# Layer 2's expert weights made beside layer 1's gathers, and layer 1's shared expert ahead of its routed experts

## The chip, the cores and the metric

The kernel runs on one core of a Trainium2 chip. The metric is the device time of one execution in microseconds (us). TensorE (PE, with its weight loads as PEld), VectorE (DVE), ScalarE (ACT), GpSimd (POOL) and SyncE (SP, which only issues DMAs) have a queue of instructions each and run side by side. All data is float32.

## The reference, cut to what matters

Four layers follow each other on an activation `x` of 4 x 1024 tokens with 128 features; each has a mixing part ("attn") and a feed-forward part ("ffn"), and a layer norm follows each part. What this case touches:

```python
# layer 1, ffn: 16 experts, 4 chosen for each token, and a shared expert of width 256
h = jnp.einsum('td,edf->etf', x, gate_w)
u = jnp.einsum('td,edf->etf', x, up_w)
y = jnp.einsum('etf,efd->etd', jax.nn.silu(h) * u, down_w)
routed = jnp.einsum('etd,te->td', y, combine)
sh = jax.nn.silu(x @ sh_gate_w) * (x @ sh_up_w) @ sh_down_w
return (routed + sh).reshape(hidden_states.shape)
...
# layer 2, ffn: 8 experts share w_gate, w_up, w_down; each adds a product of rank 16 to each of them
d1 = jnp.einsum('enr,efr->enf', jnp.einsum('nd,erd->enr', x, A1), B1) * SCALE
act = jax.nn.silu(common_w1[None] + d1) * (common_w3[None] + d3)
```

Layer 1's mixing part is a linear recurrence over 1024 steps with 128 complex states (`l1_attn` in the kernel), layer 0's ffn a product with values rounded to six bits (`l0_ffn`), layer 2's mixing part causal attention with 16 heads (`l2_attn`).

## The kernel before

The tokens lie in 32 tiles of 128, in four quarters of the sequence with 8 tiles each; `x` and its transpose `xT` stay in SBUF. The four layers are worked on for parts of the sequence. First the first half (quarters 0 and 1) goes through layer 0 and the mixing part of layer 1: `l0_attn((0, 1))`, `l0_ffn((0, 1))`, `l1_attn((0, 1))`. Then its route is computed (`l1_route`), and GpSimd scatters its rows with 64 indirect DMAs into a list in DRAM that is sorted by expert (`spread`), while `l0_attn((2, 3))` works on the second half. Layer 1's ffn of the first half follows, with `l0_ffn` and `l1_attn` of the second half as side work. Then comes `l2_attn(0)`.

The ffn of layer 1 has four pieces:
- `l1_wall` loads the 16 experts' weights, 3 MB, into one tile `wall` (line 153, the DMA issue `ld<-in_l_w` of SP).
- `l1_experts` (`small_experts`) runs over 20 groups of four tiles of the sorted list: SP loads the rows (`xg`, L1324), TensorE transposes them (`tp`, L165), multiplies with gate and up of the tile's expert (`gu`, L157), ScalarE and VectorE form the product (L1688, L1689), TensorE transposes it and multiplies with down (`yp`), and SP writes `yg` to DRAM (L1707).
- `l1_shared` runs over 4 blocks of 512 tokens: two pairs of matmuls `pg` and `pu` from `xT`, `down` as `py`, and an add into `x` (L822). It loads its own three weights of 128 KB each.
- `l1_close` collects, quarter by quarter: for each of 8 tiles GpSimd gathers four rows per token with four indirect DMAs (`yt`, L1293, five buffers of four), VectorE adds them into `x` with their weights (L1359), and then come the norm, a copy of `x` to DRAM (`xsave`, L832) and the transposes (`turned`). A gather reads rows of the whole list, so the first one waits for the last `yg`.

`l1_attn` takes one quarter after the other: two matmuls `pu` from `xT`, four products on VectorE (L641), two scans over 1024 columns (L645), the state that is carried on (L655 to L661), a product on GpSimd (L663; on VectorE where it runs as side work) and one on VectorE (L664), 16 pairs of matmuls `po`, two adds into `x` (L672), norm and transposes.

`l2_weights` makes the layer 2 weights of the 8 experts, three for each. It loads `l2_big` (1.5 MB) and `l2_ab` (192 KB). In each of 24 steps GpSimd multiplies `ab` with a column of 0 and 1 that picks the expert's 16 rows, and with 2 (`am`, L1399), TensorE adds the shared weight (by a matmul with the identity) and the product of rank 16 in PSUM (`pw`, printed as `s`), ScalarE copies it (`we`, L1409) and SP writes 256 KB to DRAM (`wall2`, L1411). `l2_wall` reads it back much later, from 843.67 us on.

The order of the work: each of these pieces is a generator that yields an estimate of its time. `mix(main, side)` takes a step of `main` and then as many steps of `side` as `main`'s estimates pay for; the `side` instructions on PE, ACT, DVE and POOL are put behind those of `main` that came before (`queued`). `chain` runs generators one after the other, and `abreast` takes the one whose estimates add up to least so far. When the program is built, a list scheduler fixes each engine's order from this; memory of a closed pool goes to the next ones, with waits. `self.side` is a PSUM pool of two buffers that `l2_weights`, `turned` and the side work share.

Before the change, `l2_weights` begins with its loads ahead of `l0_ffn((0, 1))`, and its 24 steps are the side work of `l1_attn((0, 1))`, with 1.0 as each step's estimate. The experts run ahead of the shared expert, which stands beside the gathers.

Of the kernel before, what the change touches and what calls it, by code (L numbers as in the profile page):

```python
# [14 lines left out]
AF = mybir.ActivationFunctionType  # L15
ALU = mybir.AluOpType
# [4 lines left out]
P = 128  # L21
# [20 lines left out]
E2, F2, R2, K2 = 8, 512, 16, 2  # L42
# [32 lines left out]
class Kernel:  # L75
# [1309 lines left out]
    def l2_weights(self):  # L1385

        nc = self.nc
        NC = F2 // P
        with ExitStack() as ctx:
            cp = self.pool(ctx, "l2wc", right=True)  # L1390
            wp = self.pool(ctx, "l2ww", 3, right=True)
            big = self.load(cp, self.ins["l2_big"])
            ab = self.load(cp, self.ins["l2_ab"])
            yield (0.0,)
            for e in range(E2):
                for i in range(3):

                    am = self.tile(wp, [P, P], "am")
                    nc.gpsimd.tensor_scalar(am, ab[:, i, :], self.cst["em"][:, e : e + 1], 2.0, ALU.mult, ALU.mult)  # L1399
                    pw = self.tile(self.side, [P, F2], "s")  # L1400
                    self.mm(pw, self.ident, big[:, i, :], True, False)
                    if i < 2:
                        self.mm(pw, am, big[:, 3 + i, :], False, True)
                    else:
                        for c in range(NC):
                            f = slice(c * P, (c + 1) * P)
                            self.mm(pw[:, f], big[:, 5, f], am, False, c == NC - 1)
                    we = self.tile(wp, [P, F2], "we")
                    nc.scalar.copy(we, pw)  # L1409
                    c0 = (e * 3 + i) * F2  # L1410
                    nc.sync.dma_start(out=self.wall2[:, c0 : c0 + F2], in_=we)  # L1411
                    yield (1.0,)

    def l2_route(self, part):
        nc = self.nc
# [393 lines left out]
    def all(self):  # L1809
        a, rest = self.first, self.rest  # L1810
        b, c = rest
        r = self.both[1]
        a2, m2, n2 = self.by_rows
        with ExitStack() as ctx:
            lgp = self.pool(ctx, "l2lg")
            self.l2_lg = self.tile(lgp, [P, NT, E2], "lg")
            with ExitStack() as early:

                self.l0_setup(early)
                self.l2_wr = self.load(lgp, self.ins["l2_wr"])  # L1820
                self.run(self.l0_attn((0, 1)))
                self.l1_setup()
                self.l2_setup()
                weights = self.l2_weights()
                next(weights)
                self.zero_lists("l1")
                self.run(self.l0_ffn((0, 1)))
                self.run(self.mix(self.l1_attn((0, 1)), weights))

                self.run(self.l1_route(a))  # L1830
                self.run(self.mix(self.l0_attn((2, 3), True), self.spread("l1", a, K1)))
                self.zero_lists("l2", "l3")
                with ExitStack() as c2:
                    wall = self.l1_wall(c2)
                    yp = self.pool(c2, "l1ya", 5, right=True)
                    side = self.chain(self.l0_ffn((2, 3), True), self.l1_attn((2, 3), True))
                    self.run(self.mix(self.l1_experts(a, wall), side, drain=False))
                    self.run(self.mix(self.chain(self.l1_shared(a), side), self.l1_close(a, yp)))
            with ExitStack() as c2:
                wall = self.l1_wall(c2)  # L1840
                self.run(self.mix(self.l2_attn(0), self.chain(self.l1_route(r), self.spread("l1", r, K1))))
                wall2 = self.l2_wall(c2)
                yp = self.pool(c2, "l1yr", 5, right=True)
                self.run(self.mix(self.chain(self.l1_experts(r, wall), self.l1_shared(r)), self.routed(a2)))
                self.run(self.mix(self.l2_experts(a2, wall2), self.l1_close(r, yp)))
            listed = lambda name: lambda: name in self.listed
            on = self.served(
                self.chain(self.rows_in(a2), self.onward(a, True)),
                (lambda: self.rows_done >= B + 2, self.routed(m2)),
                (lambda: self.rows_done == 2 * B, self.routed(n2)),  # L1850
            )
            self.run(self.mix(self.l2_attn(1), on, drain=False))
            with ExitStack() as c3:
                with ExitStack() as c2:
                    wall = self.l2_wall(c2)
                    self.press(on, listed("l2m"))
                    self.run(self.mix(self.l2_experts(m2, wall), on, drain=False))
                    self.press(on, lambda: {"l2n", "routed l3a"} <= self.listed)
                    sw, wall3 = self.l3_wall(c3, True)
                    on = self.chain(on, self.rows_in(m2))  # L1860
                    self.run(self.mix(self.l2_experts(n2, wall), on, drain=False))
                self.press(on, listed("l3a"))
                yp = self.pool(c3, "l3y", 8)
                on = self.chain(
                    on, self.rows_in(n2), self.l3_attn(b), self.l3_route(b),
                    self.abreast(
                        self.chain(self.spread("l3", b, K3), self.when(listed("made l3a")), self.last(a, yp)),
                        self.chain(self.l3_attn(c), self.l3_route(c)),
                    ),
                    self.spread("l3", c, K3), self.when(listed("made l3b")), self.last(b, yp),  # L1870
                )
                self.run(self.mix(self.chain(self.l3_shared(a, sw), self.l3_experts(a, wall3)), on, drain=False))
                self.press(on, listed("l3b"))
                self.run(self.mix(self.chain(self.l3_shared(b, sw), self.l3_experts(b, wall3)), on, drain=False))
                self.press(on, listed("l3c"))
                self.run(self.mix(self.chain(self.l3_shared(c, sw), self.l3_experts(c, wall3)), on))
                self.run(self.last(c, yp))
        bad = self.nc.values_load(self.flag[0:1, 0:1], min_val=0, max_val=1)
        with self.tc.If(bad > 0):
            with ExitStack() as ctx:  # L1880
                lgp = self.pool(ctx, "l2lg2")
                self.l2_lg = self.tile(lgp, [P, NT, E2], "lg")
                self.l2_wr = self.load(lgp, self.ins["l2_wr"])
                self.l2_attn_general()
                for p in self.by_rows:
                    self.run(self.routed(p))
                    with ExitStack() as c2:
                        self.run(self.l2_experts(p, self.l2_wall(c2)))
                    self.run(self.rows_in(p))
                for p in self.parts:  # L1890
                    self.run(self.onward(p))
                    with ExitStack() as c2:
                        sw, wall = self.l3_wall(c2)
                        self.run(self.l3_shared(p, sw), self.l3_experts(p, wall))
                        self.run(self.last(p, self.pool(c2, "l3y" + p.name, 5)))
# [165 lines left out]
```

## Time and profile before

| | us |
|---|---|
| median of 3 runs | 2137.66 (2135.64 to 2137.95) |
| the profiled execution | 2141.15 |
| its span, first to last instruction | 2139.3 |
| PE busy | 1624.2 (76%) |
| DVE busy | 1346.1 (63%) |
| ACT busy | 816.4 (38%) |
| POOL busy | 787.2 (37%) |
| `l1_attn((0, 1))` with the weights: first `pu` to second quarter's `po` | 211.4 to 280.4 |
| first and last gather of layer 1's first half | 545.48 and 633.43 |

Durations and positions come from the profiled execution, whose positions count from its first instruction; the median of the runs is 3.5 us below its own time. A row of a timeline has the start, the length, the engine, the line, the operation and what it writes and reads; the brackets give the idle time of the engine before it and what ended that. A busy TensorE is not TensorE at its peak, and idle time of an engine that nothing waits for costs nothing.

### The profile page before, as it was taken

Reading aid. Unit: us, or ns where it says so; the run is one execution under the profiler, and the core shown is the slowest. Engines: PE = TensorE matmul, PEld = TensorE weight load, DVE = VectorE, ACT = ScalarE, POOL = GpSimd, SP = SyncE. Lnnn points to the kernel's source line nnn. Section 1 sums busy time; section 2 is a strip of 40 time slices with the busy share of each in tenths; the row PEclk is TensorE's granted clock in tenths of the full one; section 3 lists DMA queues with packets and bytes.
Section 4 is the critical chain, followed back from the end, with each engine's and each line's share of the span. In section 5 each row is a group of like instructions: output and inputs, shape, how many; then the busy total and the mean of one; then the engine's idle time right before and its main releaser. Section 6 shows DMA issues by size and latency. Waiting matters only on the chain.

```text
span 2139.3 us, 28621 instructions
## 1 busy us (share of the span) xinstructions
PE 1624.2 (76%) x9605; PEld 1001.0 (47%) x9605; DVE 1346.1 (63%) x3797; ACT 816.4 (38%) x1162; POOL 787.2 (37%) x725
## 2 busy tenths in 40 slices
PE   6563967678618787989979787894989999577680
PEld 2232533367414345856633232333656688356470
DVE  8765379868666867536646667464573367568363
ACT  4621236433104344323347554661323254233240
POOL 5523218821560470535232000200226700477725
PEclk9775979789758999999999998996999999789795
DMA  9940300143320023633230000003134243144351
GB/s 323 289 126 1 118 2 35 59 137 94 127 55 11 30 111 104 222 82 85 59 114 23 1 1 1 21 1 138 50 115 148 82 122 100 37 127 127 114 147 50
DMA packets 224008, 192.05 MB, mean 90 GB/s; under 512 B 16817, under 2 KB 204081, under 8 KB 222833
## 3 DMA queue, kind: packets, MB, share of 16 engines
q1 hardware_dynamic: 203152, 147.28, 22.0%
q0 software_dynamic: 20704, 42.86, 6.5%
q8 instruction: 83, 1.36, 0.3%
q14 instruction: 69, 0.56, 0.1%
HBM read 93.47 MB, written 96.60 MB: 89 GB/s over the span
## 4 chain that ended last, share of the span: by engine, by line
PE 42%; DVE 16%; POOL 5%; issue 4%; DMA 4%; ACT 3%; SPq 0%; POOLq 0%; DVEq 0%; ACTq 0%
PE gu L157 12%; PE s L157 9%; PE sc L157 6%; PE yp L157 5%; PE tp L165 5%; POOL yt L1293 3%; PE pg L157 2%; POOL l3rc L1293 2%; PE pu L157 2%; DVE pr L1055 1%; POOL l3rb L1293 1%; PE py L157 1%; DVE x L205 1%; ACT pr L1049 1%; PE s L165 1%
## 5 line engine op out<-in xcount | busy, mean ns | idle before, releaser
L1049 ACT ACTIVATE pr<-sc 128x1024 f32<-128x1024 f32 x288 | 279.1, 1021 | 216.5 <-PE sc L157 216.5
L157 PE MATMUL gu<-ld,xgT 128*128 x768 | 195.0, 394 | 20.7 <-DVE hg L1689 12.6
L157 PE MATMUL sc<-qm,kT 32*128 32x512 f32 (+3 forms) x1536 | 190.2, 552 | 1.0 <-ACT pr L1049 1.0
L157 PE MATMUL gu<-wall,xgT 128*128 x352 | 170.8, 609 | 19.9 <-DMA wall<-wall 17.9
L157 PE MATMUL s<-pr,va 128*32 128x512 f32 (+3 forms) x1536 | 164.1, 522 | 17.7 <-DVE x L987 7.3
L157 PEld LDWEIGHTS gu<-ld,xgT 128*128 128x128 f32 x768 | 140.6, 194 | 49.7 <-ACT xgT L167 9.1
L1055 DVE TENSOR_TENSOR pr<-pr,ld 128x512 f32<-128x512 f32 (+1 forms) x160 | 92.3, 580 | 87.0 <-ACT pr L1049 86.6
L169 DVE COPY hT<-tp 128x512 f32<-128x512 f32 x140 | 95.7, 684 | 68.0 <-PE tp L165 67.8
L1689 DVE TENSOR_TENSOR hg<-sg,gu 128x256 f32<-128x256 f32 x192 | 77.9, 414 | 93.2 <-ACT sg L1688 92.8
L157 PEld LDWEIGHTS sc<-qm,kT 32*128 32x128 f32 x1536 | 83.0, 196 | 99.1 <-issue 62.6
L1462 ACT ACTIVATE sg<-gu 128x512 f32<-128x512 f32 x88 | 52.5, 598 | 199.4 <-PE gu L157 194.4
L1688 ACT ACTIVATE sg<-gu 128x256 f32<-128x256 f32 x192 | 73.2, 384 | 143.3 <-PE gu L157 115.4
L167 ACT COPY xgT<-tp 128x512 f32<-128x512 f32 x118 | 69.2, 586 | 142.8 <-PE tp L165 142.7
L165 PEld LDWEIGHTS tp<-ld,hg 128*128 128x128 f32 x736 | 91.8, 142 | 57.5 <-issue 35.8
L165 PE MATMUL tp<-ld,xg 128*128 128x128 f32 x472 | 77.7, 288 | 52.9 <-DMA xg<-l3rb 15.7
L165 PE MATMUL tp<-ld,hg 128*128 128x128 f32 x736 | 113.7, 274 | 4.5 <-DVE hT L169 2.9
L1293 POOL DMA_INDIRECT l1ra<-x,posl1a x64 | 94.4, 1476 | 60.9 <-DVE posl1a L1270 41.7
L1464 DVE TENSOR_TENSOR hg<-sg,gu 128x512 f32<-128x512 f32 x88 | 59.9, 681 | 74.8 <-ACT sg L1462 74.5
L157 PE MATMUL yp<-ld,hT 128*128 x768 | 102.7, 276 | 0.8 <-DVE hT L169 0.5
L1293 POOL DMA_INDIRECT l1rr<-x,posl1r x64 | 64.6, 1009 | 101.3 <-DVE posl1r L1270 82.1
L157 PEld LDWEIGHTS yp<-ld,hT 128*128 128x128 f32 x768 | 93.7, 192 | 1.7 <-DVE hT L169 0.9
L157 PE MATMUL yp<-wall,hT 128*128 x704 | 93.1, 275 | 1.5 <-DVE hT L169 1.5
(433 smaller groups left out, 3449.4 us busy)
## 6 DMA issues: line engine op xcount, KB each, us to landing
wall<-wall SPq DMA_DIRECT2D x16, 768.0 KB, 11.2
l3ra<-zero SPq DMA_DIRECT2D x1, 6144.0 KB
wall<-we SPq DMA_DIRECT2D x24, 256.0 KB, 2.0
ld<-in_l_w SPq DMA_DIRECT2D x2, 3072.0 KB, 13.0
ld<-in_l_w SPq DMA_DIRECT2D x1, 6144.0 KB, 19.8
xg<-l3ra SPq DMA_DIRECT2D x24, 256.0 KB, 3.8
l3ya<-yg SPq DMA_DIRECT2D x24, 256.0 KB, 2.3
l1ra<-zero SPq DMA_DIRECT2D x1, 5120.0 KB, 21.7
```

The costliest lines, as they stand in the source:

```text
L157: return self.nc.tensor.matmul(out, lhsT, rhs, start=start, stop=stop)
L165: nc.tensor.transpose(pt[:, k * P : (k + 1) * P], s, self.ident)
L167: nc.scalar.copy(dst, pt[:, : n * P])
L169: nc.vector.tensor_copy(dst, pt[:, : n * P])
L205: nc.vector.tensor_scalar(x, x, mv[:, t, 0:1], rstd[:, t : t + 1], ALU.subtract, ALU.mult)
L1049: nc.scalar.activation(pr, sc[h], AF.Exp)
L1055: nc.vector.tensor_tensor(d, d, cst["tril"].unsqueeze(1).unsqueeze(1).to_broadcast([P, 2, n, P]), ALU.mult)
L1293: ins = self.nc.gpsimd.indirect_dma_start(**kw)
L1462: nc.scalar.activation(sg, gu[:, 0, :], AF.Silu)
L1464: nc.vector.tensor_tensor(h, sg, gu[:, 1, :], ALU.mult)
L1688: nc.scalar.activation(sg, pg[:, :, 0, :], AF.Silu)
L1689: nc.vector.tensor_tensor(h[:, 2 * c : 2 * c + 2, :], sg, pg[:, :, 1, :], ALU.mult)
```

## The change

`l2_weights` leaves `l1_attn((0, 1))`. It now runs abreast of the rest of the second half's side work while `l1_close` gathers. Its masks go from GpSimd to ScalarE, with the factor 2 put into a column `em` that VectorE makes once, its pools go to the other end of the memory, and each step's estimate is 2.5 instead of 1.0. The shared expert of layer 1's first half leaves the gathers and runs ahead of the experts, in one chain with them, beside the side work.

```diff
-            cp = self.pool(ctx, "l2wc", right=True)
-            wp = self.pool(ctx, "l2ww", 3, right=True)
+            cp = self.pool(ctx, "l2wc")
+            wp = self.pool(ctx, "l2ww", 3)
             big = self.load(cp, self.ins["l2_big"])
             ab = self.load(cp, self.ins["l2_ab"])
+            em = self.tile(cp, [P, E2], "em2")
+            nc.vector.tensor_scalar(em, self.cst["em"], 2.0, None, ALU.mult)
...
-                    nc.gpsimd.tensor_scalar(am, ab[:, i, :], self.cst["em"][:, e : e + 1], 2.0, ALU.mult, ALU.mult)
+                    nc.scalar.activation(am, ab[:, i, :], AF.Copy, scale=em[:, e : e + 1])
...
-                    yield (1.0,)
+                    yield (2.5,)
...
-                weights = self.l2_weights()
-                next(weights)
                 self.zero_lists("l1")
                 self.run(self.l0_ffn((0, 1)))
-                self.run(self.mix(self.l1_attn((0, 1)), weights))
+                self.run(self.l1_attn((0, 1)))
...
-                    self.run(self.mix(self.l1_experts(a, wall), side, drain=False))
-                    self.run(self.mix(self.chain(self.l1_shared(a), side), self.l1_close(a, yp)))
+                    self.run(self.mix(self.chain(self.l1_shared(a), self.l1_experts(a, wall)), side, drain=False))
+                    self.run(self.mix(self.abreast(self.l2_weights(), side), self.l1_close(a, yp)))
```

## The prediction

> **What bounds the kernel now.** I read the page's 40 slices first, then the table by stage, the timeline at the stages' borders, the waits and the chain. The table comes first; its columns are the stretch in us, its length, then busy us (and instructions) of PE, PEld, DVE, ACT and POOL, the granted TensorE clock, the DMA share and GB/s.
>
> ```profile
> core 0: us, PE busy (x) PEld busy (x) DVE busy (x) ACT busy (x) POOL busy (x), PEclk, DMA share, GB/s
> 216.00:265.00 49.00, 48.02 (x188) 27.15 (x186) 17.16 (x40) 15.24 (x27) 12.73 (x22) 0.99 0.35 129
> 265.00:282.00 17.00, 7.54 (x48) 7.29 (x48) 13.11 (x32) 0.00 (x0) 3.33 (x1) 0.70 0.00 0
> ...
> 460.00:480.00 20.00, 18.25 (x125) 15.79 (x124) 17.22 (x59) 8.03 (x17) 2.36 (x1) 1.00 0.37 106
> ...
> 547.00:571.50 24.50, 24.50 (x105) 14.82 (x104) 8.80 (x17) 5.85 (x10) 17.77 (x19) 0.91 0.59 210
> 571.50:600.80 29.30, 9.94 (x43) 7.74 (x41) 26.61 (x89) 0.59 (x1) 21.38 (x18) 0.63 0.15 38
> 605.00:636.00 31.00, 2.27 (x8) 1.44 (x8) 11.47 (x42) 1.47 (x3) 22.36 (x24) 0.50 0.24 68
> ```
>
> TensorE is full from 216 to 265, where the weights are made; while the outputs of layer 1's experts are gathered (545 to 636) it is nearly empty but for the shared expert. The timeline shows what each stage waits for (start, length, engine, line; in brackets the idle time before and its releaser):
>
> ```profile
> 221.91 3.27 POOL L663 TENSOR_TENSOR g<-g,pw 128x1024 f32<-128x1024 f32 x1 [0.74 <-DVE l1h L660]
> 235.47 0.69 DVE L672 TENSOR_TENSOR x<-po,x 128x512 f32<-128x512 f32 x1 [10.27 <-PE po L157]
> 263.20 2.48 DVE L641 TENSOR_TENSOR b<-pu,wi 128x512 f32<-128x512 f32 x4 [15.80 <-PE pu L157]
> 274.77 5.62 PE L157 MATMUL po<-l1c,g 128*128 128x128 f32 x32 [7.51 <-POOL g L663]
> 423.19 0.33 SPq L153 DMA_DIRECT2D ld<-in_l_w  x1
> 437.47 1.99 PE L165 MATMUL tp<-ld,xg 128*128 128x128 f32 x8 [14.42 <-DMA xg<-l1ra]
> 545.48 1.02 POOL L1293 DMA_INDIRECT yt<-l1ya,posl1a  x1 [46.81 <-DMA ld<-in_l_swu]
> 576.72 2.92 POOL L1293 DMA_INDIRECT yt<-l1ya,posl1a  x1 [0.30 <-DMA yt<-l1ya,posl1a]
> ```
>
> The first and last lines will serve below. Between them: VectorE, which carries `l1_attn`, waits 10.27 us for `po` and 15.80 us for the second quarter's `pu`, both behind weight matmuls in TensorE's queue. Then TensorE waits 14.42 us for the first experts' rows. The chain of waits confirms the later bound, and shows one load that comes late behind others:
>
> ```profile
> 633.43 2.49 DMA yt<-l1ya,posl1a
> ...
> 859.76 6.33 DMA xg<-l1rr
> ```
>
> GpSimd's 64 gathers, the last at 633.43, release the norm after which `l2_attn(0)` starts.
>
> **The change, part by part.** All positions are those of the profiled execution (2141.15 us, span 2139.3).
>
> *Weights out of `l1_attn(0, 1)`.* A weight step takes four 128x512 matmuls 0.43 us apart, or two and eight of 0.11, so 1.72 to 1.75 us; 24 make 41.4 us, gone from 216 to 265. What is late next is `l1_attn`'s own chain. GpSimd's product ends at 225.2 (221.91 + 3.27), so the first quarter's `po` starts there and not at 233.5, on a cold clock (5.6 us for 32, the row at 274.77). The second quarter's `pu` needs only `xT` and the two PSUM buffers that L641 frees at 216.4; its VectorE work (2.5 for L641, 4.6 for two scans, 1.1 for the carried state) then runs from 223, with the first quarter's adds and statistics (3.6) between, to about 235. GpSimd's product adds 3.3: the second `po` starts near 238.5 instead of 274.77, **-36 us**. Everything up to the experts hangs on this chain (route, scatters, `l0_attn(2, 3)`) and moves along. Bounds: the two quarters wholly one after the other put it at 250.9 (13.1 us of tail after 225.2, then 12.6 from `pu` to `po`, as before), -24; an overlap without any loss, -38. I take -36, because before, too, instructions ready early ran early (zeroing of layer 3's lists at 75, ahead of `l0_ffn`'s weight load).
>
> *Shared expert ahead.* Its 24.3 us (547.1 to 571.4, first matmuls at half clock) should fall into the 14.4 us gap, but its weights are loaded after the 3 MB of `l1_w`, issued at 423.19 when `gate` is free. In the one-microsecond table that load moves about 400 GB/s until 433.7. In the row at 859.76 a load behind eight of 768 KB took 6.33 us against its median 3.2, so I let the 384 KB land after it, at 434.7. The shared expert then runs from 434.7 to 459, and the experts start 21.5 us later than 437.5. Bounds: its weights ahead of `l1_w`, start near 423, +10; no overlap with any wait, +24.
>
> The Trainium skill's page "DMA: Bandwidth & Descriptors", section "Queues, rings and completion order", speaks against this step: on each DMA engine the descriptors of one issuer's row are consumed in ring order. By it the gap stays empty, as I have it; a queue that shared its rate evenly would land the 384 KB about 2 us after issue and save some 9 us.
>
> *Experts and the side work.* The experts now run with the end of `side`: the shared expert's four steps advance it by 22 units, so at the experts' end 99.7 of 108 units are issued, not 77.7. Work from 435 to 600.8, summed over the table's stretches: PE 128.0 us, some 6 of it from cold clocks, so 122; DVE 122.1, less 11.1 of gathered adds and `l2_attn`'s memsets, so 111. From 460 to 530 PE was busy for 64.0 of 70 us (0.915), DVE for 60.2 (0.86). So PE gives 133 us and DVE 129: the end is at 566 to 568. Two engines that are both this full wait for each other a little more; I take 569 against 541.2, **+28 us**. Bounds: PE at 1.00 (557, +16); DVE at the whole stage's 0.79 (81.7 of 103.7; 577.5, +36).
>
> *Gathers.* They start 4.3 us after the last expert, as before (541.2, 545.48). Undisturbed, from 609.7 to 633.4, they are 1.25 us apart, 79.7 us for 64. They took 88.9: 4.0 us waiting for an add queued behind the shared expert on VectorE, the rest beside `l1_attn`'s last quarter, where single ones took 1.9 to 2.9. Both causes leave. I take 82, **-7 us** (0 to -9.2).
>
> The last timeline row is a gather of 2.92 us while VectorE scans (2.28 us, started at 576.60). The Trainium skill's page "SBUF — State Buffer", section "SBUF: two separate sides", says of the port pair that VectorE and GpSimd share that it is an exclusive lock, held for the whole instruction, so that a DMA issued by GpSimd starves for descriptors. By that rule alone only the overlapped gathers get shorter, some 5 us, not 7.
>
> *Weights beside the gathers.* 41.4 us of PE in about 82 where, without the shared expert, PE has some 13 us to do. ScalarE's mask lies between 0.302 us (128x8, L195) and 1.13 (128x1024, scaled by a column, L432), by length 0.40; with the 0.59 of the copy (L1409) 24 steps are 23.8 us on an engine busy for under 10. GpSimd, which the gathers need, gets none of it. Writes: 6.3 MB. Cost nothing; the load of 1.7 MB adds about 6 us before the first step. At half clock the steps would be 83 us and end 7 us after the gathers; before, they ran at 0.99. `em` is one 128x8 operation, about 0.16 us. The waits that are added: matmuls of `turned` and `side` share two PSUM buffers with the weights, and on SP `xsave` stands behind the weights' writes; both have 30 us to spare.
>
> *Loads off the start.* 1.7 MB less before the zeroing: nothing, as the next load, issued at 112.27, lands 18.7 us later and is read at 157.6. The 24 masks leave GpSimd (0.37 each): nobody waited but for 0.8 us.
>
> Sum: -36 + 28 - 7 = **-15 us**, 2126 us against 2141.15. The median shown, 2137.66, is 3.5 below the profiled execution: 2123.
>
> **The rivals.**
> *The gap is filled.* If the shared expert's weights land first, it starts up to 11.5 us earlier: -26, 2111. For it: their memory is free before `gate` is; against it: text order. Chance 0.13.
> *The weights were not the bound.* If the second quarter of `l1_attn` stays behind the first one's norm, the gain is 24: -24 + 28 - 7 = -3, 2135, no change. For it: at 208.5 to 211.4 `pu` of the first quarter was ready and yet waited for transposes; against it: that was a wait for memory in PSUM, which doesn't exist here. Chance 0.13.
> *The gathers lose their pace* (the slower side). Masks, copies, 24 writes and transposes now meet 64 gathers that have five buffers; if each takes what the scatters took beside a busy VectorE (L1293, 1.476 + 0.30 between), the train is 114 us, not 88.9: -36 + 28 + 25 = +17, 2155. It decides from 1.51 us per gather on, (88.9 + 8)/64; with a mean of 1.55 it is +2. Against it: scatters at 424 to 429, beside the 400 GB/s of `l1_w`, kept 1.26. Chance 0.14.
>
> **How the numbers follow.** My forecast has 0.60, its own range 2113 to 2134 (the bounds +16 to +36 narrowed by half, and some of the first term). For 8 in 10 the range takes in most of the first rival and the near part of the last: 2108 to 2142. A measurement can tell 0.2%, 4.3 us, from no change. Faster: nearly all of 0.60, the 0.13 and a little of the second rival, 0.73; the same 0.13; slower 0.14.
>
> **What would show it.** After: no `am` on POOL and no weight matmuls before 260; the second `po` near 238; the scatters, and the load of `l1_w`, 36 us earlier; the shared expert's first matmul about 11 us after that load's issue; the last expert product about 8 us earlier than 541; gathers 1.25 us apart, the last near 618; weight matmuls done some 25 us before that. I am wrong if `po` stays near 250, if the experts end later than 541, or if the gathers exceed 90 us.

## The result, and the profile after

The changed kernel takes 2141.41 us (median of 20 runs, 2132.90 to 2145.23) against 2134.47 for the one before (20 runs, 2128.01 to 2140.06): a ratio of 1.0030, 95% interval 1.0022 to 1.0039. It is slower by about 7 us; the forecast was 15 us faster.

The two first profiles seem to say the opposite: 2141.15 us for the profiled execution of before, 2136.98 for that of after. Each is untypical of its kernel, the one above all 20 timed runs, the other third from the bottom. So the stages are compared first, and a second profile of each kernel (below) tells which of them repeat. The table of after by stretches comes first, in columns like those of before:

```profile
core 0: us, PE busy (x) PEld busy (x) DVE busy (x) ACT busy (x) POOL busy (x), PEclk, DMA share, GB/s
205.00:241.00 36.00, 20.03 (x72) 13.96 (x71) 29.22 (x61) 2.65 (x5) 6.54 (x2) 0.61 0.00 0
393.00:400.00 7.00, 0.00 (x0) 0.00 (x0) 0.12 (x2) 0.00 (x0) 1.91 (x2) 0.50 0.93 375
400.00:432.00 32.00, 25.98 (x102) 15.68 (x103) 18.50 (x22) 5.36 (x9) 9.46 (x4) 0.89 0.06 17
...
605.00:629.00 24.00, 0.00 (x0) 0.00 (x0) 8.54 (x29) 0.00 (x0) 16.58 (x18) 0.50 0.19 51
629.00:640.00 11.00, 8.52 (x26) 4.85 (x26) 6.04 (x26) 2.54 (x5) 0.00 (x0) 0.68 0.42 149
```

In the first row TensorE is no longer full, as meant. In the second it does nothing for 7 us, and VectorE next to nothing (0.12 us), while DMA runs at 375 GB/s. In the row of 605 it does nothing again, for 24 us, although weights are still to be made: they are made from 629 on, when the gathers are over. The timeline of after shows why (columns as before):

```profile
207.50 6.35 PE L157 MATMUL pu<-xT,ld 128*128 128x512 f32 x8 [0.68 <-ACT xT L167]
241.00 6.63 PE L157 MATMUL po<-l1c,g 128*128 128x128 f32 x32
388.43 0.33 SPq L153 DMA_DIRECT2D ld<-in_l_w  x1
388.81 0.42 SPq L153 DMA_DIRECT2D ld<-in_l_swg  x1
400.09 2.08 PE L157 MATMUL pg<-xT,ld 128*128 128x512 f32 x2 [11.79 <-DMA ld<-in_l_swg]
435.01 1.04 PE L165 MATMUL tp<-ld,xg 128*128 128x128 f32 x8
535.14 0.50 SPq L153 DMA_DIRECT2D ld<-in_l_w  x1
538.49 0.36 SPq L1709 DMA_DIRECT2D l1ya<-yg  x1
547.06 1.02 POOL L1293 DMA_INDIRECT yt<-l1ya,posl1a  x1 [82.50 <-DMA w<-in_l_w]
590.68 0.30 ACT L195 ACTIVATE rstd<-mv,eps 128x8 f32<-128x8 f32 x1 [1.67 <-DVE mv L192]
625.81 0.94 POOL L1293 DMA_INDIRECT yt<-l1ya,posl1a  x1 [0.30 <-issue]
628.34 0.35 DVE L1359 SCALAR_TENSOR_TENSOR x<-yt,wkl1a,x 128x128 f32<-128x128 f32 x1 [0.86 <-DMA yt<-l1ya,posl1a]
629.36 2.14 DVE L205 TENSOR_SCALAR x<-x,mv,rstd 128x128 f32<-128x128 f32 x8
629.85 2.18 PE L165 MATMUL s<-ld,x 128*128 128x128 f32 x8 [36.36 <-DVE x L205]
637.62 0.59 ACT L1411 COPY we<-s 128x512 f32<-128x512 f32 x1 [1.49 <-PE s L157]
638.10 0.30 ACT L195 ACTIVATE rstd<-mv,eps 128x8 f32<-128x8 f32 x1
638.68 2.14 DVE L205 TENSOR_SCALAR x<-x,mv,rstd 128x128 f32<-128x128 f32 x8
```

Three rows of before, for comparison: the issue of the same second load of 3 MB (the last write of the experts' outputs was issued ahead of it, at 542), the last add of a gathered row, and the second quarter's norm.

```profile
544.71 0.59 SPq L153 DMA_DIRECT2D ld<-in_l_w  x1
636.01 0.35 DVE L1359 SCALAR_TENSOR_TENSOR x<-yt,wkl1a,x 128x128 f32<-128x128 f32 x1 [0.67 <-DMA yt<-l1ya,posl1a]
639.56 2.13 DVE L205 TENSOR_SCALAR x<-x,mv,rstd 128x128 f32<-128x128 f32 x8
```

Read the rows of after from the top. Both quarters' `pu` run in one go, and the second `po` comes at 241.0 and not at 274.8. The 3 MB of `l_w` are issued at 388.43 and not at 423.19. The shared expert's first weight is issued right behind them, and its first matmul waits 11.79 us for it. It then takes 31 us, to 431, so that the first experts start at 435.01, against 437.47 before: of the gain of 34 us at the last scatter (394.56 against 429.14) nearly nothing is left. Near 535 a second load of 3 MB, for the second half's experts, is issued ahead of the last write of the experts' outputs. The first gather comes 8.6 us after that write's issue; before it was 3.5 us. The brackets name `w`, a load that landed with it on the same queue; what a gather needs is the write.

The last eight rows are the end. ScalarE has the first quarter's root at 590.98, but VectorE normalises that quarter only at 629.36: in its queue the normalisation stands behind all of the second quarter's adds. TensorE has the first quarter's transposes ahead of the last two weight steps in its queue, so it waits 36.36 us; SP has that quarter's save ahead of the last three weight writes. ScalarE has the second quarter's root behind the last weight copy, so that quarter's norm comes at 638.68, 10 us after its last add at 628.34. Before, it came 3.5 us after the last add.

The next table gives the stages as differences of such rows, in us: from the second norm of layer 0 (at 155.6 before, 152.1 after) to the last scatter; to the experts' last `yp`; to the first gather; to the last one; to the first scores `sc` of `l2_attn(0)`; and their sum. The rows from the third on are the experiments.

| kernel | scatter | `yp` | first gather | last gather | `sc` | sum | ratio to before, 95% |
|---|---|---|---|---|---|---|---|
| before, two profiles | 273.5, 273.4 | 112.0, 112.0 | 4.4, 4.4 | 88.0, 88.8 | 20.2, 18.5 | 498.0, 497.1 | 1 |
| after, two profiles | 242.5, 242.1 | 143.0, 143.0 | 9.5, 9.8 | 78.8, 78.9 | 26.5, 26.0 | 500.2, 499.8 | 1.0030 (1.0022 to 1.0039) |
| weights_only | 242.4 | 111.6 | 4.5 | 105.4 | 17.3 | 481.2 | 0.9932 (0.9912 to 0.9952) |
| shared_only | 271.5 | 142.8 | 9.8 | 78.9 | 16.3 | 519.3 | 1.0155 (1.0133 to 1.0178) |
| norm_dve | 244.0 | 143.3 | 10.2 | 78.9 | 32.3 | 508.8 | 1.0058 (1.0038 to 1.0079) |
| shared_early_load | 243.1 | 131.7 | 8.5 | 78.9 | 26.9 | 489.1 | 0.9964 (0.9949 to 0.9979) |
| pace_1_5_b | 243.5 | 143.3 | 9.9 | 79.0 | 19.4 | 495.1 | 1.0009 (0.9993 to 1.0024) |
| last_write_act_b | 242.1 | 143.0 | 14.8 | 78.7 | 25.8 | 504.4 | 1.0053 (1.0033 to 1.0072) |
| early_pace_write_b | 242.2 | 129.7 | 14.6 | 79.0 | 21.7 | 487.2 | 0.9960 (0.9943 to 0.9976) |
| wall_behind | 243.3 | 141.9 | 4.3 | 78.8 | 26.3 | 494.6 | 0.9999 (0.9984 to 1.0014) |
| early_pace_behind | 244.1 | 130.1 | 4.3 | 78.8 | 21.6 | 478.9 | 0.9917 (0.9892 to 0.9942) |

### The profile page after: what moved, and what is told of

Same layout as the page of the kernel before. It is cut to its first block, busy times and chain, and to the rows that moved or that the text cites. A ratio compares the mean times of both kernels' runs of the same rounds, so it can differ in the third digit from the quotient of the medians.

```text
span 2135.1 us, 28614 instructions
## 1 busy us (share of the span) xinstructions
PE 1621.9 (76%) x9605; PEld 999.8 (47%) x9605; DVE 1352.8 (63%) x3798; ACT 823.4 (39%) x1186; POOL 767.6 (36%) x701
## 4 chain that ended last, share of the span: by engine, by line
PE 43%; DVE 16%; POOL 7%; issue 6%; DMA 4%; ACT 3%; SPq 0%; POOLq 0%; DVEq 0%; ACTq 0%
PE gu L157 12%; PE s L157 10%; PE yp L157 6%; PE sc L157 6%; PE tp L165 5%; POOL yt L1293 4%; POOL l3rc L1293 2%; DVE pr L1055 1%; POOL l3rb L1293 1%; ACT pr L1049 1%; PE pg L157 1%; PE pu L157 1%; PE s L165 1%; DVE x L205 1%; PE py L157 1%
## 5 line engine op out<-in xcount | busy, mean ns | idle before, releaser
L1293 POOL DMA_INDIRECT yt<-l1ya,posl1a x64 | 60.5, 945 | 101.7 <-DMA w<-in_l_w 82.5
```

Of the source, the lines that this page charges most:

```text
L1293: ins = self.nc.gpsimd.indirect_dma_start(**kw)
```

## The experiments

The theory from the two traces: the gain at the scatters is real; it is lost in three places, of which the forecast had only the first. The shared expert stands in the open, waiting for its weights; the gathers start behind a 3 MB load; the last weight steps stand behind the first quarter's closing in three queues. The rivals: moving the weights is itself the loss, or the end of the weights isn't on the path.

**Each part alone.** `weights_only` leaves the shared expert beside the gathers; `shared_only` is the kernel before with the shared expert ahead of the experts.

```diff
 weights_only, against after
-self.run(self.mix(self.chain(self.l1_shared(a), self.l1_experts(a, wall)), side, drain=False))
-self.run(self.mix(self.abreast(self.l2_weights(), side), self.l1_close(a, yp)))
+self.run(self.mix(self.l1_experts(a, wall), side, drain=False))
+self.run(self.mix(self.abreast(self.l2_weights(), self.chain(self.l1_shared(a), side)), self.l1_close(a, yp)))
 shared_only, against before
-self.run(self.mix(self.l1_experts(a, wall), side, drain=False))
-self.run(self.mix(self.chain(self.l1_shared(a), side), self.l1_close(a, yp)))
+self.run(self.mix(self.chain(self.l1_shared(a), self.l1_experts(a, wall)), side, drain=False))
+self.run(self.mix(side, self.l1_close(a, yp)))
```

> The weights are made beside the gathers, with ScalarE's masks, as in the changed kernel; the shared expert stays in its old place, beside the gathers too. Theory (the shared expert in the open is what eats the gain of 34 us that the last scatter shows): the scatters come some 34 us earlier than before, the experts follow at once and end near 508, and beside the gathers TensorE has 24 + 41 us of 89 to do, so the gathers stay at some 89 and a tail of up to 10 us is lost at their end. Time 20 to 30 us below before, near 2108. Rival (moving the weights is itself what loses, because they disturb the gathers and the norm behind them): less than 8 us below before, or above it.

> The shared expert goes ahead of the experts; the weights stay beside the first half's layer 1 attention, with GpSimd's masks. Theory: the shared expert costs its 24 to 31 us in the open, less about 9 us of faster gathers: 15 to 24 us above before, near 2153. Rival (the shared expert fills the gap before the first experts' rows, and so costs under 15): no more than 6 us above before. The two parts alone should add up to the whole change: with the sum far from +7 us, they share a cost.

Measured: 2117.74 us and 2163.65, before beside them 2132.64. The weights alone gain 15 us, less than the 20 to 30 of the theory, far from the rival. The shared expert alone costs 31 us, more than either expectation. The stages show both: the scatters' 31 us come with the weights, the 31 us up to `yp` with the shared expert. Together the parts give +16 by the medians, against +7 for the whole, and by the table's sums +5.3 (481.2 and 519.3 against 497.6) against +2.4. Of the 31 us of `shared_only` the table's stages hold 21.7. The rest isn't located; its profiled execution, at 2157.12 us, is the shortest of its five runs. In `weights_only` the gathers take 105.4 us, 17 more than before, since weights, shared expert and `l1_attn`'s scans now lie beside them at once:

```profile
557.56 0.94 POOL L1293 DMA_INDIRECT yt<-l1ya,posl1a  x1 [18.98 <-DVE x L1359]
566.29 2.49 POOL L1293 DMA_INDIRECT yt<-l1ya,posl1a  x1 [0.30 <-issue]
```

These two rows of its timeline are a wait of 18.98 us for a buffer, whose add stands behind the shared expert's adds in VectorE's queue, and a gather of 2.49 us beside a scan that started at 565.74. That wait alone is as long as the 17 us. So the whole is cheaper than its parts at this place, and each part's price holds only with its neighbours.

**The shared expert's weights, loaded early.** They are loaded behind `l2_setup` into a pool of their own, and passed on.

```diff
                 self.l2_setup()
+                sp = self.pool(early, "l1sw")
+                got = [self.load(sp, self.ins["l1_" + n]) for n in ("swg", "swu", "swd")]
...
-self.chain(self.l1_shared(a), self.l1_experts(a, wall))
+self.chain(self.l1_shared(a, got), self.l1_experts(a, wall))
```

> The changed kernel with one edit: the shared expert's 384 KB are loaded at the start of the kernel's second stage, into memory of their own, and not behind the 3 MB of the experts' weights. Theory (TensorE and VectorE both stand idle from 393 to 400 for these 384 KB): the shared expert's first matmul comes 6 to 9 us earlier, near 392, and all that follows with it; 6 to 9 us less than the changed kernel, near 2134. Rival (the experts' rows or weights are late anyway and eat it): within 2 us of the changed kernel, with the first experts still near 435.

Measured: 2125.24 us, 0.9964; that is 14 us less than the changed kernel by the ratios, twice what was expected, and 7 less than before. The first row of its timeline:

```profile
394.11 1.25 PE L157 MATMUL pg<-xT,ld 128*128 128x512 f32 x2
```

It stands 4.4 us ahead of the last scatter (398.55), in after 5.5 us behind it (400.09 against 394.56), so it comes 10 us sooner, where 6 to 9 were expected. The shared expert then takes 24 us, to 418, and not 31. It still meets the rounding of `l0_ffn` on VectorE, but loses less by it: TensorE waits 0.47 and 1.84 us for `hs` products queued behind rounding steps, where in after it waits 2.90 and 2.59. Its first two matmuls take 1.25 us and not 2.08. The rest of the difference isn't broken down. The stage up to `yp` gets 11.3 us shorter. So the forecast had the empty gap rightly, at 11.5 us.

**The end of the weights, first by the norm.** In the first half's `l1_close`, `norm` gets `by="dve"`.

```diff
-            self.norm(self.quarter(q))
+            self.norm(self.quarter(q), by="dve" if part is self.first else "act")
```

> The changed kernel with one edit: in the first half's closing of layer 1, the norm takes its inverse root on VectorE (Newton steps, some 14 short operations of 0.2 us) and not by ScalarE's root. Theory (the tail: the first quarter's normalisation stands at 629 behind all of the second quarter's adds, the last weight steps stand behind its transposes, and ScalarE's root of the second quarter behind the last weight copy): the first quarter is normalised near 597, the last weight matmuls run soon after, the second quarter is normalised some 4 us after its last add and not 10; 5 to 7 us less than the changed kernel, near 2135. Rival (the tail is not on the path, something else sets the start of the next attention): within 2 us of the changed kernel.

Measured: 2143.02 us, 1.0058, no gain; if anything a loss. The norms came about as expected (602.41 and 633.77, the second one 4 us after the last add), but the weights did not. SP's part of the timeline tells why:

```profile
556.61 14.43 SPq L1413 DMA_DIRECT2D wall<-we  x8
604.56 0.32 SPq L832 DMA_DIRECT2D xsave<-x  x1
604.98 5.11 SPq L1413 DMA_DIRECT2D wall<-we  x5
```

The order of each queue is fixed when the kernel is built. Here the first quarter's save stands behind eight of the 24 weight writes and holds up the next eight until the quarter is normalised, and the second quarter's save, at 635.94, does so to the last eight. The three buffers `we` fill, ScalarE waits 32.08 us for one of them, TensorE for ScalarE. So this edit put the same fault in another queue: it was no test of the rival, and the next one was made.

**The end of the weights, by their pace.** A step counts 1.5 units and not 2.5, so all 24 are issued ahead of the first quarter's closing, in every queue.

```diff
-                    yield (2.5,)
+                    yield (1.5,)
```

> The changed kernel with one number changed: a weight step counts 1.5 units and not 2.5, so that all 24 steps are issued ahead of the first quarter's closing, and none stands behind its transposes, its save or its norm in the queues of TensorE, SP and ScalarE. The order of VectorE (the first quarter's normalisation behind all adds) stays. Theory (the tail of the weights in these queues costs 6 to 7 us between the last gather and the next attention): weight matmuls end near 600, the second quarter's norm comes some 5 us after its last add and not 10; 4 to 7 us less than the changed kernel, near 2135. Rival (the norm on VectorE tried before showed that only other steps then stand in the way, so the tail is a matter of the total work and not of its place): within 2 us of the changed kernel.

> The same kernel as pace_1_5, whose chip ran every kernel, the one before too, 18% slower and with stalls of 10 to 70 us in which the profile shows no work. Expected as there: theory, weight matmuls end near 600, the second quarter's norm some 5 us after its last add and not 10, 4 to 7 us less than the changed kernel (ratio to before 0.9995 to 1.001, from the changed kernel's 1.003); rival, the ratio stays at 1.003 or above.

The first chip was disturbed: there before took 2526.58 us, every kernel had stalls of tens of us, and a second profile of before (`before_again`, 2527.33 us) had them too. The ratios of the three changed kernels that ran on it, 1.0062 for this one, 1.0065 for `last_write_act` and 1.0059 for `early_pace_write`, are not used here for differences of 5 us. On the second: 2133.27 us, 1.0009. Its interval, 0.9993 to 1.0024, still overlaps that of the changed kernel, 1.0022 to 1.0039; the profile is clearer:

```profile
633.38 2.14 DVE L205 TENSOR_SCALAR x<-x,mv,rstd 128x128 f32<-128x128 f32 x8
635.66 2.14 DVE L205 TENSOR_SCALAR x<-x,mv,rstd 128x128 f32<-128x128 f32 x8
```

The last weight matmul starts at 598.1 and not 637.3. Both norms follow the last add (630.42), the second one 5.2 us after it and not 10. From the last gather to the scores 19.4 us pass, as in before (20.2 and 18.5), not 26.5. The rival falls: the end of the weights was on the path, with about 7 us of the stage, 4.5 by the ratios. The other rows of the table agree: where the last weight step comes ahead of the last gather, the stage to `sc` takes 16.3 to 21.7 us, where it comes behind it, 25.8 to 32.3.

**The start of the gathers, first by another queue.** The last write of `yg` is issued by ScalarE and not by SP.

```diff
-                nc.sync.dma_start(
+                queue = nc.scalar if part is self.first and lay == "l1" and g == ng - 1 else nc.sync
+                queue.dma_start(
```

> The changed kernel with one edit: the last write of the experts' outputs is issued on ScalarE's DMA queue and not on SP's, where it stands behind the 3 MB load for the second half's experts. Theory (the gathers start 8.6 us after that write's issue, and not 3.5 as before, because of that load): the first gather comes 4 to 5 us earlier, near 542, and 3 to 5 us are saved at the end, near 2137; it may also lose part of this if the transfers share their rate and not their order. Rival (the gathers wait for something else, or the rate is shared): first gather within 1.5 us of 547, time within 2 us of the changed kernel.

> The same kernel as last_write_act. There the first gather came 17.5 us after the write's issue, later than with the write on SP's queue (7.6 us in the kernel beside it): the transfers shared their rate and the write got little of it. So now: theory of the ring order, first gather 4 to 5 us earlier than 547 and ratio to before 1.0005 to 1.001; rival, the write shares the rate with the 3 MB in front of it wherever it is issued, the gathers start no earlier than 547, ratio 1.003 or above.

(The 17.5 us in the second text are 12.4 by the trace: issued at 547.79, first gather at 560.17. It is still later than with the write on SP.) Measured on the undisturbed chip: 2142.50 us, 1.0053; the first gather came at 551.79, 13.8 us after the write's issue and 4.7 us later than in after. The expectation failed in its sign. The table of DMA queues, for 543 to 549 us, shows how the two queues shared:

```profile
q1 hardware_dynamic: 337, 2.23, 89.7%
q10 hardware_dynamic: 339, 0.17, 9.5%
```

The columns are packets, MB and the time of the packets as a share. In these 6 us SP's queue (q1, the loads) and ScalarE's (q10, the write) moved as many packets, 337 and 339, but the write's are of 512 bytes and it got 0.17 MB of 2.40. In this stretch the two queues shared by packets and not by bytes; from 542 to 543 it was 16 packets each, and before 541 none of the write had moved, which was issued at 537.96. The Trainium skill's page "DMA: Bandwidth & Descriptors", section "Queues, rings and completion order", says that each DMA engine goes round the queues it has work for at packet granularity; the equal counts above fit that. A packet of the page can hold several descriptors, and no run here shows whether the profile counts the same unit. The page says, too, that on each engine the descriptors of one queue are consumed in ring order. The 8.6 us of after agree with that: there the write stood whole behind the 3 MB.

**The start of the gathers, by the order.** The load for the second half's experts is put behind that of `l2_ab` on SP, by a dependency in the builder and without a wait on the chip.

```diff
             ab = self.load(cp, self.ins["l2_ab"])
+            self.behind = self.traced[n:][-1].name
...
                 wall = self.l1_wall(c2)
+                for i in self.traced[n:]:
+                    self.tc.add_manual_dep(i, self.behind, DependencyInfo(NoSync, DATA), reason="queued behind")
```

> The changed kernel with one edit: the 3 MB load for the second half's experts is put behind the loads of the weights' inputs in SP's queue, and so behind the experts' last write too; before, both stood behind it. Theory (on one queue a transfer waits for all that was issued ahead of it): first gather 3.5 us after the last write's issue and not 8.6, first weight matmul near 545 and not 551, 4 to 5 us less than the changed kernel: ratio to before 1.0005 to 1.001. Rival (the rate is shared, as the write on the other queue showed, and 3 MB hurt wherever they lie): first gather no more than 2 us earlier, ratio 1.002 or above.

Measured: 2131.98 us, 0.9999 (0.9984 to 1.0014), some 6.6 us less than the changed kernel by the ratios. SP's queue and the first gather in its timeline:

```profile
537.86 0.36 SPq L1711 DMA_DIRECT2D l1ya<-yg  x1
538.31 0.46 SPq L153 DMA_DIRECT2D ld<-in_l_big  x1
538.86 0.40 SPq L153 DMA_DIRECT2D ld<-in_l_ab  x1
539.31 0.44 SPq L153 DMA_DIRECT2D ld<-in_l_w  x1
541.25 1.02 POOL L1293 DMA_INDIRECT yt<-l1ya,posl1a  x1 [77.32 <-DMA l1ya<-yg]
```

The write lands 3.4 us after its issue, as in before, and the brackets now name it. The first weight matmul starts at 545.75, in after at 551.05. The gathers keep their pace beside the 3 MB (78.8 us). The rival of the shared rate falls for one queue.

**All together.** Early load and pace with the write on ScalarE's queue, then with the order instead.

> The changed kernel with all three edits: the shared expert's weights loaded early, a weight step at 1.5 units, the last write on ScalarE's queue. Theory (three separate losses, one after the other on the path): the savings add up, 15 (measured for the early load) + 5 + 4, so some 20 to 25 us less than the changed kernel, near 2118 or below, level with or below the kernel with the weights alone. Rival (they overlap: one that is removed uncovers the next): no more than 3 us below the early load alone, 2122 or above.

> The same kernel as early_pace_write. Theory: savings of 15 (early load) and 5 (pace) add up, the write's is in doubt; 18 to 20 us less than the changed kernel, ratio to before near 0.994. Rival: no better than the early load alone, 0.9964 or above.

> The changed kernel with three edits: the shared expert's weights loaded early, a weight step at 1.5 units, the 3 MB load behind the weights' inputs. Theory: the three losses lie one after the other, so the savings of 14 (early load, by medians), 4.5 (pace) and 5 (load order) add up to some 22 us less than the changed kernel, near 2118 with before at 2133, ratio 0.992 to 0.994; level with the weights alone (0.9932). Rival (they overlap): 0.996 as with the write on ScalarE's queue.

With the write: 2122.71 us, 0.9960, no better than the early load alone, since the gathers start 14.6 us after the last `yp`. With the order: 2115.36 us, 0.9917 (0.9892 to 0.9942). The single edits were worth 14, 4.5 and 6.6 us by their ratios, 25 in all; together they give 24. So the losses lie one after the other. This version beats both kernels; from the weights alone (0.9932, 0.9912 to 0.9952) it can't be told apart.

**How far a profile can be trusted.** Both kernels were profiled again.

> The kernel before, unchanged, for a second profile on an undisturbed chip. If its first profile (2141, above all 20 timed runs) was long by chance, this one lies near 2134 and is shorter in stretches that the change doesn't touch: up to 155 us by some 3 us, as in the profile on the disturbed chip, and from 640 to 1007 by some 4 us. Rival: the same 2139 again.

> The changed kernel, unchanged, for a second profile. The first one (2137) lies near the lowest of 20 timed runs (median 2141), and before's first near its highest. Theory: the stretch up to the second norm at 152 or 155.5 us and the one from the next attention's first scores to 1000 vary from run to run by some 3 and 8 us in either kernel, the stages between repeat within 1 us: last scatter 242.5 after that norm, experts' end 143 later, first gather 9.5, last gather 78.8, next attention 26.5. Rival: the stages of the change vary too, by 3 us or more.

The second profile of before is of 2132.65 us, that of after 2138.07. The stages of the table repeat within 0.4 us but for the last two (0.8 and 1.7 in before). What differs in before lies behind them: from the first scores to a norm near 1000 it took 353.3 us, then 347.5, and 345.9 to 353.5 in the profiles of the other kernels of the table, all with the same instructions there. The first part of this expectation failed: the second norm came at 155.5 again. In both profiles of after it came at 152.1, in the others between 150.7 and 155.5. It isn't the load taken off the start: `weights_only`, without that load, has 155.2, `shared_only`, with it, 152.5. So the 3.4 us that after's first profile gains there are not counted to the change, and what sets them stays open.

## Why the prediction was wrong

Step by step, the forecast and the measured differences of the table's stages (mean of two profiles each):

| step | forecast | measured |
|---|---|---|
| weights out of `l1_attn((0, 1))`, to the last scatter | -36 | -31.2 |
| shared expert ahead, to the last `yp` | +28 | +31.0 |
| start of the gathers | 0 | +5.3 |
| gathers | -7 | -9.6 |
| last gather to `l2_attn(0)` | 0 | +6.9 |
| sum | -15 | +2.4 |

*The step that failed* is *Weights beside the gathers*, put down as "Cost nothing", with the reason that the matmuls of `turned` and `side`, and `xsave`, "have 30 us to spare". The work fits, as it said: 41 us of TensorE in 79, ScalarE at 43% from 547 to 600, the gathers 1.25 us apart. But the steps were not looked at in their places in the queues. The forecast had the weights done 25 us before the last gather; two steps stood behind the first quarter's transposes on TensorE (and three writes behind its save on SP), the transposes behind its norm, and the norm behind all adds on VectorE. The last weight matmul started at 637.3, 11 us after the last gather. It cost 6.9 us, and `pace_1_5_b` gave it back. The forecast asked who waits behind the weights, and not behind whom the weights wait.

It is the largest of several misses and not all of the error. Between -15 and +2.4 lie 17.4 us: 6.9 of this step, 5.3 at the gathers' start, 4.8 and 3.0 by which two terms were mis-sized, less 2.6 that the gathers gained. Without the first two, if their savings by the ratios add up (4.5 and 6.6), the change would be some 4 us faster than before and not 15.

*The gathers' start.* "They start 4.3 us after the last expert, as before" did not count a load that the change moves: in before the next 3 MB were issued at 544.71, behind the last write at 542; in after, at 535.14, ahead of it. It cost 5.3 us, and `wall_behind` gave it back (4.3 us from the last `yp` to the first gather, as in before). The forecast had used the ring's order for one load of SP's queue and not gone through the others.

*Weights out* was right in its mechanism and 5 us too large. The first `po` started at 221.21, when GpSimd's product ended (217.90 + 3.26), and the second quarter's `pu` ran at once. But the second quarter's scans came behind the first quarter's adds, for which VectorE waited 2.48 us, and its statistics, and its normalisation (2.13 us) came ahead of the rest of the carried state. So the second product on GpSimd began 19.8 us after the first and not some 13. Had I taken the middle of my bounds, -31, it would have been hit; the reason I gave for the end of the range (early instructions ran early) held for TensorE, not for VectorE, which was busy for 29.2 of these 36 us.

*Shared expert ahead* was within its bounds, in part by luck. The gap of 11.5 us stayed empty, as forecast (11.79 measured). From the shared expert's first matmul to the last `yp` 137.5 us passed, where the forecast had 134 (434.7 to 569). The shared expert took 31 us instead of 24.3, and the experts' first transposes came 3.7 us behind it; the experts made up for most of that, with 103 us from there on instead of 110. Two sums in that passage are off: counted from 435, VectorE's 129 us end at 564 and not at 566, and its bound lies at 576 and not at 577.5; the +28 doesn't rest on them. By the forecast's own terms this step cost 28 us to gain 7, and without it (`weights_only`) the kernel is 15 us faster than before.

*Gathers* were right, and a little better than forecast: without the shared expert's adds and `l1_attn`'s scans all 64 were 1.25 us apart. The rival in which they lose their pace has no support in after; in `weights_only` they do take 17 us longer, mainly by a wait for VectorE (18.98 us) and less by their own pace. The rule that the prediction cites on the shared port pair holds, by the same page, for VectorE operations in a two-port mode, and for those with two inputs in SBUF only against a GpSimd operation that reads SBUF; no run here shows whether a scan is one of them.

The stages sum to +2.4 us where the medians say +7. The rest, some 4.5 us, isn't located: the stretches behind the first scores vary by up to 8 us from run to run, and two profiles of each kernel can't show a difference of 4 there.

## What to carry to other kernels

When work is moved beside other work, go through each queue that it enters and ask both questions: who stands behind it, and behind whom does it stand. Free time of the engines is worth nothing to a step that is queued behind an instruction which waits for the end of the stage. A moved stage also moves the loads behind it: look for the small write or load on the critical path that now stands behind megabytes which are needed much later (here first used at 832.75, 298 us after their issue), and put these behind it in the same queue rather than the small one on another queue. And a gain upstream is only worth something where the next stage can take it: here 31 us at the scatters went, to the microsecond, into a shared expert in the open, 11 of them into the wait for its weights.

## What the runs showed of the hardware that was not expected

Two DMA queues shared by packets while both had work under way: 339 packets of the write and 337 of the loads in 6 us, 0.17 MB against 2.23. A 256 KB write in 512 byte packets, alone on its queue, landed 13.8 us after its issue beside 3 MB and more of loads; behind the 3 MB on the same queue it took 8.6 us, ahead of them 3.4.

A gather that started while VectorE scanned took 2.49 us (in `weights_only`), one beside ScalarE's masks and copies 0.94, with the DMA at 185 GB/s from 547 to 600. The two profiles of a kernel repeat within 0.4 us in each stage up to the first gather; those of before differ by 5.8 us in a stretch of 350 us behind the first scores, those of after by 0.6.
